# A graph layer on one core: q in two float32r pieces for its spread, x plus beta made in the prologue, and the root from logarithm and exponential

## The chip, the cores and the metric

The kernel runs on one NeuronCore of a Trainium2 chip. The core has a matrix engine (TensorE, "PE", with its weight loads as "PEld"), three other compute engines (VectorE "DVE", ScalarE "ACT", GpSimd "POOL"), a sync engine ("SP") that only issues transfers, and 16 DMA engines. Each engine runs its own instructions in order, and they meet by semaphores. The metric is the device time of one execution in microseconds, as the median of several runs.

## The reference

There are 12500 nodes with 256 features and 200000 edges, sorted by destination. `h` is the normalised and rectified `x`; a layer of attention over the edges, with 8 heads of 32, is made from `h`:

```python
h = jnp.maximum(_layernorm(x, axis=-1), 0.0)
q, k, v = h @ Wq + bq, h @ Wk + bk, h @ Wv + bv      # (n, 8, 32) each
logits = jnp.einsum('ehd,ehd->eh', q[dst], k[src]) / jnp.sqrt(jnp.float32(D))
expv = jnp.exp(logits - jax.ops.segment_max(logits, dst, num_segments=n)[dst])
attn = expv / jax.ops.segment_sum(expv, dst, num_segments=n)[dst]
agg = jax.ops.segment_sum(attn[:, :, None] * v[src], dst, num_segments=n)
y = h + jax.nn.gelu(agg.reshape(n, HID) + (h @ Wskip + bskip), approximate=False)
out = x + (y - mean(y)) / jnp.sqrt(var(y) + 1e-05) * gamma + beta
```

(Two lines are drawn together here; the order of the work is the reference's.)

## The kernel before

**Prologue** (`project`, about the first 200 us). The rows of `x` are loaded in groups of up to four blocks of 128 rows (`load`, L201, five tiles `x_in`, on SP's queue). DVE takes the statistics of each block (L227, L232), ACT their root (L235), DVE its reciprocal and the shift (L239, L240), ACT the normalised rows `h` (L249). After the last block of a group `normalise` stores `h` to `h_tab` (L252) and issues the next load, into the tile that this group leaves. TensorE transposes `h` (L261) and multiplies it with the weights of k and v (L349) into `ps_kv` (four tiles); DVE adds the bias (L357), and a group's rows go to `kv_tab` (L359). Between these, POOL, DVE and ACT work off a plan of the edges (`make_plan`) and smaller tables (`aside`); `pieces` (L126) there splits a bias row into three bf16 rows `b_q3`, `b_s3` and `b_o3`, the last for `beta`.

**Walk** (`walk_streams`). The edges are cut into eight streams, and a step `c` walks three tiles of 128 edges of each. In a step and tile:

- `gather` and `gather_row` (L1504) fetch rows of k and v by 24 indirect DMAs a step, issued by POOL. Each is tied to a place in TensorE's order by `turns`.
- `turn_windows` (L1466, L1470) transposes a window of 64 rows of `h` for each stream; `queries` (L1480 to L1487) makes `q` for it in two parts, in a PSUM tile `ps_hot`, and ACT copies it to `qw`.
- `hot_e` (L1529, L1532) makes a matrix of zeros and ones, `to_e`, from edges to window rows.
- `spread` (L1555) multiplies `to_e` with `qw` in float32, so that each edge has its `q`. Two matmuls of 64 rows each stand side by side in the array. The result, `ps_qe`, has two tiles.
- DVE multiplies `q` with k (`times`, L1566), adds over a head (`total`, L1573), TensorE turns the logits (`turn`, L1592), DVE scans the running maxima (`maxima`, L1604 and L1605), ACT takes the exponential (L1608), TensorE turns back (L1614), DVE weighs v (`weigh`, L1640), and TensorE adds the products of a node (`add_up`, L1663).

The 16 most frequent nodes are done densely (`Dense`, L1820 to L1879) from step 2 to step 50.

**Finishing pairs** (`Pair`). From step 15 on, a step fetches the sums of two blocks of nodes that are done, and the next two steps finish them: division (L1225), the skip product (L1237), the sums added on TensorE (L1242), GELU on ACT (L1246), `h` added and the statistics (L1249 to L1258), the root on ACT (L1262), reciprocal and shift on DVE (L1266, L1267), the normalised rows on ACT (L1272), times gamma (L1306). `shifted` (L1299, L1302) makes `x` plus `beta` in a `ps_hot` tile by a matmul of `b_o3` and two with the identity, and DVE adds it (L1308). The four last pairs (`Half`) are finished after the loop in an order of their own, with `raised` (L1283) in place of `shifted` for some.

**The order** of every engine in the walk is the program's: `keep` chains each instruction behind the one before it on its engine. All PSUM tiles of `turn_windows`, `queries`, `hot_e`, `hot_n`, `shifted`, the dense part and some of `add_up` come from one pool, `ps_hot`, with two tiles. ACT's functions come from tables; `table_of` (L1420) loads one early by an activation on a dummy: GELU, then Sqrt, then Exp for each pair.

## Time and profile before

| | us |
|---|---|
| median of 3 runs | 2697.09 |
| lowest, highest | 2688.44, 2704.12 |
| the profiled execution | 2722.66 |
| its span, first to last instruction | 2721.1 |
| mean granted TensorE clock | 0.833 |
| HBM read, written | 505.52 MB, 81.63 MB |

The profile is of one execution, which took 1% longer than the median of the runs. "Busy" is the time in which an engine works on an instruction; the idle time before an instruction is named with the semaphore event that ended it, and "remote" stands where the profile knows no instruction for that event. The records of matmuls have modelled ends.

### The profile page before, as it was taken

What the parts mean: (1) busy time and instruction counts of PE and PEld (TensorE: products, weight loads), DVE (VectorE), ACT (ScalarE), POOL (GpSimd) and SP (SyncE); (2) the same over time, 40 slices, a digit from 0 to 9 for tenths busy, and PEclk for the clock granted to TensorE, in tenths of its full rate; (3) what the DMA queues carried; (4) which work ended last, traced back from release to release, by engine and by line L of the source; (5) the groups of instructions that cost most, each with busy time, mean ns of one, the idle gap of its engine ahead of it and who ended that gap; (6) DMA issues with size and microseconds to landing.
All of it is one profiled execution on the core that took longest, in us unless ns stands there. A gap on an engine that the chain in (4) does not pass through costs nothing. (4 is left out here: it accounts for less than half of the span.)

```text
span 2721.1 us, 38398 instructions
## 1 busy us (share of the span) xinstructions
PE 2093.9 (77%) x10881; PEld 1272.9 (47%) x10881; DVE 1915.3 (70%) x2373; ACT 1204.8 (44%) x2789; POOL 1591.6 (58%) x1744
## 2 busy tenths in 40 slices
PE   9994667776777778877878877787887777767776
PEld 4443444444444445544544444454554444444444
DVE  8885666666676667767766776666777766777776
ACT  5652233332334445445444544444545444444444
POOL 5457466666666556555555655555555555666664
PEclk9997688888788788878887887878888878887778
DMA  9777566766767677767777777767777776777774
GB/s 351 293 273 220 155 200 207 211 206 207 204 209 214 204 215 224 214 208 232 220 210 206 224 213 208 221 204 207 224 221 212 224 213 203 220 225 222 222 214 113
DMA packets 275205, 589.91 MB, mean 217 GB/s; under 512 B 60643, under 2 KB 133400, under 8 KB 272038
## 3 DMA queue, kind: packets, MB, share of 16 engines
q0 software_dynamic: 125344, 409.89, 51.4%
q1 hardware_dynamic: 148416, 176.36, 20.5%
q8 instruction: 89, 1.46, 0.2%
q10 hardware_dynamic: 1222, 1.11, 0.1%
q14 instruction: 134, 1.10, 0.1%
HBM read 505.52 MB, written 81.63 MB: 216 GB/s over the span
## 5 line engine op out<-in xcount | busy, mean ns | idle before, releaser
L1504 POOL DMA_INDIRECT kv<-kv_tab,idx x1472 | 1401.8, 952 | 981.9 <-issue 335.9
L1555 PE MATMUL ps_qe<-qw,to_e 64*128 64x256 f32 x3040 | 589.3, 501 | 34.1 <-DVE kv L1566 25.4
L1566 DVE TENSOR_TENSOR kv<-ps_qe,kv 128x1024 f32<-128x1024 f32 x380 | 451.5, 1217 | 147.2 <-remote 91.4
L1555 PEld LDWEIGHTS ps_qe<-qw,to_e 64*128 64x128 f32 x3040 | 403.5, 249 | 126.6 <-issue 45.5
L1640 DVE TENSOR_TENSOR vw<-ps_x,kv 128x2048 f32<-128x2048 f32 x188 | 427.0, 2271 | 49.7 <-ACT vw L1629 16.6
L1573 DVE TENSOR_REDUCE L<-kv 128x64 f32<-128x2048 f32 x190 | 433.9, 2283 | 4.8
L1484 PE MATMUL ps_hot<-w_q,hwT 128*128 128x256 f32 x768 | 251.3, 475 | 18.5 <-issue 9.9
L1663 PE MATMUL ps_a<-vw,to_n 128*32 128x264 f32 (+1 forms) x2232 | 228.4, 435 | 44.6 <-issue 25.3
L1532 ACT ACTIVATE to_e<-ps_hot,ones 128x384 f32<-128x384 f32 x256 | 146.9, 581 | 255.1 <-remote 96.9
L1487 ACT COPY qw<-ps_hot 128x256 f32<-128x256 f32 (+1 forms) x128 | 60.6, 474 | 344.0 <-PE ps_hot L1484 113.4
L1484 PEld LDWEIGHTS ps_hot<-w_q,hwT 128*128 128x128 f32 x768 | 165.6, 230 | 86.3 <-ACT hwT L1470 34.0
L1663 PEld LDWEIGHTS ps_a<-vw,to_n 128*32 128x32 f32 (+1 forms) x2232 | 88.7, 125 | 245.9 <-issue 194.3
L349 PE MATMUL ps_kv<-w_kv,hT 128*128 128x512 f32 x392 | 184.3, 593 | 0.7 <-ACT hT L263 0.7
L1420 ACT ACT_TABLE_LOAD x142 | 182.2, 1283 | 2.6
L1529 PE MATMUL ps_hot<-et,near 48*128 48x384 bf16 x256 | 94.1, 368 | 102.1 <-issue 84.8
L1614 PE MATMUL ps_x<-ident,W 64*128 64x64 f32 x189 | 28.9, 270 | 179.4 <-ACT hT L1222 113.9
L1470 ACT COPY hwT<-ps_hot 128x256 f32<-128x256 f32 (+1 forms) x128 | 61.2, 478 | 233.7 <-PE ps_hot L1466 129.5
L1604 DVE TENSOR_TENSOR_SCAN ps_x<-pen,ps_x 64x384 f32<-64x384 bf16 x63 | 60.6, 961 | 147.6 <-PE ps_x L1592 79.2
L1866 DVE TENSOR_TENSOR kv<-ps_hot,kv 128x256 f32<-128x256 f32 x49 | 20.8, 425 | 181.1 <-PE ps_hot L1862 100.3
L1680 ACT COPY kv<-ps_a 1x264 f32<-1x264 f32 x372 | 137.3, 369 | 4.5
L1545 ACT ACTIVATE to_n<-ps_hot,ones 128x384 f32<-128x384 f32 x189 | 108.6, 576 | 62.8 <-PE ps_hot L1542 44.9
L1614 PEld LDWEIGHTS ps_x<-ident,W 64*128 64x128 f32 x189 | 19.2, 161 | 210.6 <-ACT hT L1222 132.0
(437 smaller groups left out, 3029.3 us busy)
## 6 DMA issues: line engine op xcount, KB each, us to landing
kv<-kv_tab,idx POOLq DMA_INDIRECT x1520
kv_tab<-kvo SPq DMA_DIRECT2D x23, 1024.0 KB
hw<-h_tab SPq DMA_DIRECT2D x256, 64.0 KB
table<-sums_w SPq DMA_DIRECT2D x252, 61.9 KB
kv<-h_tab SPq DMA_DIRECT2D x98, 128.0 KB
sums<-table SPq DMA_DIRECT2D x94, 132.0 KB
h<-h_tab SPq DMA_DIRECT2D x94, 128.0 KB
x_f<-in_x_dram SPq DMA_DIRECT2D x94, 128.0 KB
```

The source lines that it names most:

```text
L349: nc.tensor.matmul(ps_kv, hT[:, c, :], w_kv[:, c, :], start=c == 0, stop=c == KC - 1)
L1420: keep(nc.scalar.activation(dummy[:, 1:2], dummy[:, 0:1], function))
L1484: keep(nc.tensor.matmul(ps[:, b, :], g["hwT"][:, b, k, :], w_q[:, k, :], start=False, stop=k == KC - 1, skip_group_check=True))
L1504: ins = nc.gpsimd.indirect_dma_start(out=t[:, s, :], out_offset=None, in_=kv_tab[:, :], in_offset=bass.IndirectOffsetOnAxis(ap=idx[:, s, j ...
L1532: keep(nc.scalar.activation(step[c]["to_e"][:, i, :], ps[:, :CH], AF.Relu, scale=-1.0, bias=ones))
L1545: keep(nc.scalar.activation(step[c]["to_n"][:, j, :], ps, AF.Relu, scale=-1.0, bias=ones))
L1555: keep(nc.tensor.matmul(ps[:, b, a, :], g["to_e"][r, 2 * half + a, j * P:(j + 1) * P], g["qw"][r, (half + a) * half, :], start=True, stop= ...
L1566: keep(nc.vector.tensor_tensor(k, g["qe", half].rearrange("p b a d -> p a b d"), k, op=OP.mult))
L1573: keep(nc.vector.tensor_reduce(g["L"][:, j, :].rearrange("p (s h) -> p s h", s=S), g["kv"][j][:, :, :HID].rearrange("p s (h d) -> p s h d" ...
L1640: keep(engine.tensor_tensor(t[:, :, HEADS:].rearrange("p s (h d) -> p s h d", h=HEADS), wj[:, :, :, None].to_broadcast([P, t.shape[1], HEA ...
L1663: keep(nc.tensor.matmul(ps[at:at + w, :], g["to_n"][:, j, i * P + at:i * P + at + w], g["vw"][j][:, s, :], start=j == 0, stop=j == tiles_o ...
L1680: keep(copy(step[c + 1]["kv"][0][0:1, s, HID - HEADS:], ps[at:at + 1, :]))
```

## The change

Three things are changed.

- **q in two pieces.** `queries` copies `q` to a float32r tile, which keeps fewer bits than float32. A new function, `remainders`, multiplies this piece with minus the identity into the PSUM tile that still holds `q`, so that what the first piece lacks is left, and copies that as a second float32r piece. `to_e` is made in float32r, and `spread` adds up two float32r matmuls in place of each float32 one. `qw` has a tile for each part, with two buffers each. `remainders` stands behind `hot_e(c + 2, 0)` for the first part and behind `hot_e(c + 2, 1)` for the second.
- **x plus beta in the prologue.** Once a group of `x` is normalised, POOL adds `beta` to it in place and stores it to a new table in HBM, `xb_tab`, from its own queue. The walk reads `xb_tab` where it read `x`; `shifted`, `raised`, `b_o3` and the late load of `beta` go.
- **The root.** `root` takes the logarithm and then the exponential of minus half of it, in place of Sqrt and a reciprocal on DVE (`inverse` goes too). Both come from one table, together with the Exp of `maxima`. `table_of` loads a table by its name, without a dummy; a pair has two loads, GELU's and, right behind the GELU, the other.

```diff
@@ normalise
                     nc.sync.dma_start(h_tab[starts[g] * P:(starts[g] + n) * P, :]
                                       .rearrange("(p b) d -> p b d", p=P), h_of[g])
+                    nc.gpsimd.tensor_add(x_in[g], x_in[g],
+                                         beta_all[:, None, :].to_broadcast([P, n, HID]))
+                    nc.gpsimd.dma_start(xb_tab[starts[g] * P:(starts[g] + n) * P, :]
+                                        .rearrange("(p b) d -> p b d", p=P), x_in[g])
                     for _ in range(1 + (g == 1) * (5 - 3)):
                         load()
@@ Pair
         def root(self):
-            self.keep(nc.scalar.activation(self.rstd, self.mv[:, :, 1], AF.Sqrt, bias=eps))
+            self.keep(nc.scalar.activation(self.rstd, self.mv[:, :, 1], AF.Ln, bias=eps))
+            self.keep(nc.scalar.activation(self.rstd, self.rstd, AF.Exp, scale=-0.5))
...
-            self.keep(nc.vector.reciprocal(self.rstd, self.rstd))
...
-        def shifted(self):
-
-            self.xb = hot_ps.tile([P, 2, HID], F32, name="ps_hot")
-            self.keep(nc.tensor.matmul(self.xb, one_row, twice(b_o3), start=True, stop=False,
-                                       skip_group_check=True))
-            for b in range(2):
-                self.keep(nc.tensor.matmul(self.xb[:, b, :], ident, self.x[:, b, :], start=False,
-                                           stop=True, skip_group_check=True))
...
-            self.keep(then.tensor_add(self.y, self.g, self.xb))
+            self.keep(then.tensor_add(self.y, self.g, self.x))
@@ table_of
-            keep(nc.scalar.activation(dummy[:, 1:2], dummy[:, 0:1], function))
+            keep(nc.scalar.preload_act_table_set(name))
+
+        GELU, EXP = "gelu_and_others", "natural_log_exp_and_others"
@@ queries
-                g["qw"] = hold.tile([P, 3, HID], F32, name="qw")
+            g["qw", part] = hold.tile([P, 2, n, HID], F32R, name=f"qw{part}", bufs=QBUFS[part])
...
-            keep(nc.scalar.copy(g["qw"][:, tiles, :], ps))
+            keep(nc.scalar.copy(g["qw", part][:, 0], ps))
+            g["rest"] = ps
+
+        def remainders(c, part):
+
+            g = step[c]
+            ps = g.pop("rest")
+            keep(nc.tensor.matmul(ps, less, g["qw", part][:, 0], start=False, stop=True,
+                                  skip_group_check=True))
+            keep(nc.scalar.copy(g["qw", part][:, 1], ps))
@@ spread
-                for b in range(2):
-                    r = slice(b * WN, (b + 1) * WN)
-                    keep(nc.tensor.matmul(ps[:, b, a, :],
-                                          g["to_e"][r, 2 * half + a, j * P:(j + 1) * P],
-                                          g["qw"][r, (half + a) * half, :], start=True, stop=True))
+                for i in range(2):
+                    for b in range(2):
+                        r = slice(b * WN, (b + 1) * WN)
+                        keep(nc.tensor.matmul(ps[:, b, a, :],
+                                              g["to_e"][r, 2 * half + a, j * P:(j + 1) * P],
+                                              g["qw", half][r, i, a * half, :], start=i == 0,
+                                              stop=i == 1))
@@ the loop of steps
             if before:
                 before.factors()
                 before.normal()
-            if before:
-                before.shifted()
...
             hot_e(c + 2, 0)
+            remainders(c + 2, 0)
...
             if pair:
                 pair.gelu()
+                table_of(EXP)
...
             if pair:
-                table_of(AF.Sqrt)
                 pair.root()
-                table_of(AF.Exp)
             queries(c + 2, 1)
             hot_e(c + 2, 1)
+            remainders(c + 2, 1)
```

The tables, `beta`'s rows and `inverse`/`raised` are changed in the same way behind the loop; a matmul with `less`, minus the identity in float32r, is what `remainders` uses.

More of the change, by code (lines that the diff above doesn't have):

```diff
@@ L30 @@
 F32 = mybir.dt.float32
+F32R = mybir.dt.float32r
 BF16 = mybir.dt.bfloat16
@@ L467, in gnn_kernel @@
         walk_streams(tc, N, HID, NST, KL, many, ident, idx, d0_row, slot_row, near, near_n, e_tab, pen_tab,
[L468 to L469 removed]
+                     h_tab, kv_tab, table, xb_tab, out, w_q, w_s, one_row, b_q3, b_s3,
+                     gam, eps, run_tab, cnt_tab, own, Wk, bk, Wv, bv)
     with branch.Else():
@@ L1113, in walk_streams @@
 def walk_streams(tc, N, HID, NST, KL, many, ident, idx, d0_row, slot_row, near, near_n, e_tab, pen_tab, h_tab,
-                 kv_tab, table, x, out, w_q, w_s, one_row, b_q3, b_s3, b_o3, gam, beta, eps,
+                 kv_tab, table, x, out, w_q, w_s, one_row, b_q3, b_s3, gam, eps,
                  run_tab, cnt_tab, own, Wk, bk, Wv, bv):
@@ L1398, in walk_streams @@
         nc.vector.memset(low0, -BIG)
+        less = one.tile([P, P], F32R, name="less")
+        nc.scalar.activation(less, ident, AF.Copy, scale=-1.0)
         pin = one.tile([P, 2 * P + 2], F32, name="pin")
```

58 lines of the change are left out of this document (19 added, 39 removed).

## The prediction

> **What bounds the kernel now.** I read the page first, its busy shares and its row of granted clock, then the window sums by stage, then VectorE's groups with their waits, and last the timeline of one step.
>
> ```profile
> span 2721.1 us, 38398 instructions
> PE 2093.9 (77%) x10881; PEld 1272.9 (47%) x10881; DVE 1915.3 (70%) x2373; ACT 1204.8 (44%) x2789; POOL 1591.6 (58%) x1744
> 1511.17 0.95 POOL L1504 DMA_INDIRECT kv<-kv_tab,idx  x1 [0.30 <-issue]
> ```
> No engine is full. In the window sums (columns: length, then busy time and count of PE, weight loads, DVE, ACT, POOL, then granted clock, DMA share, GB/s) I take two windows of the prologue, then the steps without a pair of finished blocks, then most of those with one:
>
> ```profile
> 0.00:100.00 100.00, 96.55 (x309) 48.48 (x310) 83.74 (x278) 60.85 (x145) 63.50 (x117) 1.00 0.93 339
> 100.00:200.00 100.00, 100.00 (x330) 48.44 (x328) 84.87 (x267) 61.66 (x144) 44.73 (x68) 1.00 0.77 277
> 347.00:821.00 474.00, 338.98 (x1889) 206.17 (x1881) 315.65 (x248) 159.97 (x416) 295.75 (x313) 0.82 0.70 206
> 821.00:2200.00 1379.00, 1084.34 (x5772) 671.85 (x5772) 978.67 (x1067) 652.25 (x1484) 796.17 (x836) 0.83 0.73 216
> ...
> L1605 DVE TENSOR_TENSOR_SCAN M<-pen,ps_x x14: 954/955/956, 347.3 to 821.0; 64x384 f32<-64x384 bf16 x14
> L1605 DVE TENSOR_TENSOR_SCAN M<-pen,ps_x x36: 954/955/956, 821.0 to 2213.4; 64x384 f32<-64x384 bf16 x36
> ```
> The prologue is TensorE's (96.55 and 100 of 100 us). The scan of L1605 comes once a step, so a step takes 473.7/13 = 36.4 us without a pair and 1392.4/35 = 39.8 us with one. In the last window PE is 79% busy, DVE 71%, and one gather takes 0.95 us of POOL and 0.30 to the next (the timeline's row above: start, length, what, idle before), 24 of them 30 us. So a step is a loop of waits between engines of similar load. DVE has the most work that can't be moved, so I price the change by what it does to DVE's waits. Its groups from 800 to 2400 us (40 steps), busy and mean, then idle time before them:
>
> ```profile
> L1566 DVE TENSOR_TENSOR kv<-ps_qe,kv 128x1024 f32<-128x1024 f32 x244 | 290.0, 1218 | 68.7 <-remote 44.3 <-PE ps_hot L1529 23.4 <-issue 0.9
> L1604 DVE TENSOR_TENSOR_SCAN ps_x<-pen,ps_x 64x384 f32<-64x384 bf16 x40 | 38.5, 961 | 92.0 <-PE ps_x L1592 68.8 <-PE ps_qe L1555 22.2 <-PE ps_hot L1466 0.9
> L1249 DVE TENSOR_TENSOR sums<-sums,h 128x512 f32<-128x512 f32 x39 | 27.0, 693 | 75.9 <-ACT hwT L1470 37.6 <-ACT sums L1246 19.3 <-issue 18.9
> L1306 DVE TENSOR_TENSOR sums<-sums,gam 128x512 f32<-128x512 f32 x38 | 26.3, 692 | 55.0 <-ACT sums L1272 48.8 <-issue 6.2
> L1866 DVE TENSOR_TENSOR kv<-ps_hot,kv 128x256 f32<-128x256 f32 x36 | 15.3, 425 | 124.0 <-PE ps_hot L1862 58.1 <-PE ps_qe L1555 56.5 <-issue 6.2
> ```
> A step waits 1.7 us for gathers and PE (L1566), 2.3 for the scan's transposes (L1604), 1.9 for the GELU's result (L1249), 1.4 for the normalised rows (L1306) and 3.1 for the dense transposes (L1866).
>
> **The change, part by part.** *Beta's matmuls go (L1299, L1302).* One step around the wait for the scan:
>
> ```profile
> 1528.70 0.58 PE L1299 MATMUL ps_hot<-b_o,one_row 3*128 3x512 bf16 x1 [2.36 <-ACT to_e L1532]
> 1529.22 2.07 PE L1302 MATMUL ps_hot<-x_f,ident 128*128 128x256 f32 x4
> 1531.22 3.79 PE L1555 MATMUL ps_qe<-qw,to_e 64*128 64x256 f32 x16
> 1535.28 0.27 PE L1592 MATMUL ps_x<-ident,L 128*64 128x128 f32 x1
> 1535.59 0.96 DVE L1604 TENSOR_TENSOR_SCAN ps_x<-pen,ps_x 64x384 f32<-64x384 bf16 x1 [3.48 <-PE ps_x L1592]
> ...
> L1299 PE MATMUL ps_hot<-b_o,one_row x47: 371/579/604, 893.5 to 2710.8; 3*128 3x512 bf16 x47
> L1302 PE MATMUL ps_hot<-x_f,ident x180: 379/634/796, 893.9 to 2623.6; 128*128 128x256 f32 x180
> ```
> TensorE does beta (0.58 us) and x (2.07), then two spreads (3.79), then the transpose for which the scan has waited 3.48 us. Overlaps taken off, the first two are 2.5 us here; I take 2.2 for the mean step, since the fast form of the records (371 and 379 ns) is also seen. They also hold one of the two ps_hot tiles.
>
> *The spread in float32r (L1555).* What TensorE takes for it:
>
> ```profile
> L1555 PE MATMUL ps_qe<-qw,to_e 64*128 64x256 f32 x3040 | 589.3, 501 | 34.1 <-DVE kv L1566 25.4
> 1511.64 0.73 PEld L1555 LDWEIGHTS ps_qe<-qw,to_e 64*128 64x128 f32 x8 [0.30 <-DVE kv L1566]
> 1511.65 1.13 PE L1555 MATMUL ps_qe<-qw,to_e 64*128 64x256 f32 x8
> ```
> Four calls a spread on 380 spreads make 1520 matmuls, and the trace has 3040: a float32 matmul is two records. A record with 256 float32 columns lasts as long at its shortest as one with 512 bf16 columns (379 and 371 ns), so each record runs at half bf16's pace. No float32r row exists. If a call is one record at bf16's pace, eight calls stand where eight records stood at half the length each: about 0.5 us less of the 1.13 of a spread. If it is one record at the old pace, nothing changes; if it stays two records, a spread costs about 1.0 us more. The weight loads stay eight, 0.73 us, and may then set the pace, so I take 0.3 us a spread, between the first two. Of six spreads in a step, two lie ahead of the scan's transpose and one ahead of L1862. The other three end while DVE does other work and count nothing; if that cover goes, they add 0.9 us to the gain.
>
> *The second piece of q.* Twice a step comes a matmul with minus the identity and a second ACT copy out of the same ps_hot tile.
>
> ```profile
> 1517.47 0.37 ACT L1487 COPY qw<-ps_hot 128x256 f32<-128x256 f32 x1 [5.51 <-remote]
> 1517.74 0.59 ACT L1532 ACTIVATE to_e<-ps_hot,ones 128x384 f32<-128x384 f32 x1
> 1517.90 1.01 PE L1466 MATMUL ps_hot<-ident,hw 128*128 128x128 f32 x4 [2.72 <-ACT qw L1487]
> ...
> 1519.43 0.60 ACT L1246 ACTIVATE sums<-ps_a 128x512 f32<-128x512 f32 x1
> ```
> Now L1466 starts when the first copy is out. Afterwards it also waits for the remainder's matmul, the 0.59 us activation ahead of it on ACT, and a copy like the 0.37 us one: about 0.9 us later. Behind L1466 on TensorE stand the transpose of L1592 and the second half of q; behind its result on ACT stands the GELU (L1246), and DVE's L1249 waits for that, so this 0.9 us is on the path with a pair. The same round trip for the second half stands ahead of the last spread; I put it at nothing with a pair, because qw's copy comes earlier (next part), and at 0.9 if that fails. Bounds for both trips together: nothing, and 3 us (two copies, the matmul near 0.4 us and the handovers, twice).
>
> *The root.* Three table switches a pair become two, and Sqrt with a reciprocal becomes Ln and Exp.
>
> ```profile
> L1420 ACT ACT_TABLE_LOAD x142 | 182.2, 1283 | 2.6
> L1420 ACT ACTIVATE dummy<-dummy 1x1 f32<-1x1 f32 x142 | 28.7, 202 | 1.6
> L1262 ACT ACTIVATE rstd<-mv,eps 128x2 f32<-128x2 f32 x47 | 13.9, 295 | 11.8 <-DVE mv L1258 4.8 <-issue 4.1 <-DVE st L1256 3.0
> L1266 DVE RECIPROCAL rstd<-rstd 128x2 f32<-128x2 f32 x46 | 7.1, 155 | 0.0
> ```
> ACT loses 1.28 us and three dummies of 0.20, and gains one activation near 0.30: 1.6 us less, of which the two new copies (0.37 and 0.59) take back 0.96. The load behind the root is gone, so qw's second copy follows the statistics 1.2 us sooner, and the normalised rows come some 0.3 us earlier for L1306. DVE loses 0.16 us outright. [...]
>
> *The prologue.* All of x gets beta on POOL and is written once more, 12.8 MB, from POOL's queue.
>
> ```profile
> L1283 POOL TENSOR_TENSOR x_f<-x_f,kv x2: 1264/1268/1272, 2661.6 to 2684.4; 128x512 f32<-128x512 f32 x2
> L1362 POOL DMA_DIRECT2D kv<-in_x_dram x16 | 8.5, 553 | 0.3
> L349 PE MATMUL ps_kv<-w_kv,hT 128*128 128x512 f32 x392 | 184.3, 593 | 0.7 <-ACT hT L263 0.7
>   DMA x_in<-in_x_dram: 5.6, 5
> POOL kv L1492 <- PE ps_hot L1529: 16.8, 1, 16.8
> ```
> An addition over 512 columns took 1.27 us, so one over 1024 takes 2.5, and the 25 groups about 62 us, with 25 issues of 0.55 us (14 us). POOL was idle 92 us in the first 200 and waited 16.8 us at the end, so it has room. But a load of x now waits for the addition and the store of the group five before it, 5 us or more behind plan work. The last but one row is from the waits of L227, the statistics: they waited only 5.6 us for such loads, which come just in time; behind a waiting L227 on DVE stand the evictions of L357, and TensorE has four tiles before it stops. Behind the load on SP stand the stores of h and of keys and values. DMA is 0.93 and 0.77 busy. Bounds: nothing, and 12.8 MB at 339 GB/s unhidden, 38 us. I take 12, nearer the free end because four tiles of 1.9 us (184.3 us for 98 blocks) cover one late load.
>
> *The end.* Four additions of 1.27 us on POOL, beta's DMA and the last two pairs' matmuls go: 2 us, between 0 and 8.
>
> **The sum.** With a pair: beta's matmuls 2.2 and two spreads 0.6 make 2.8, but the scan's wait is 2.3, so 2.3; the third spread 0.3, L1306 0.3, the reciprocal 0.16; against them 0.9 at L1249. That is 2.16 off. Gathers are next: their waits (1.1 us of L1566's 1.7) grow as steps shorten, and I give 0.26 back: 1.9. Without a pair: 0.6 + 0.3 off, 0.5 on for round trips without the GELU: 0.4. So 46 x 1.9 = 87, 16 x 0.4 = 6, the end 2, the prologue +12: 83 us less. The profiled execution itself took 2722.7 us (span 2721.1), so 2640 on its scale. The median of the three runs is 2697.09, 26 less; the same 83 us off gives **2614**.
>
> **The rivals.** *TensorE is the real bound* (chance 0.15). For: 79% busy, and only 8.5 us a step left. Then beta's 2.2 and six spreads' 1.8 less two 0.15 us matmuls count in full, 3.7 a pair step and 1.5 otherwise: 46 x 3.7 + 16 x 1.5 = 194, less 12: 2515. Against: the waits of DVE for ACT and gathers do not shrink with it.
>
> *The gathers take it all* (0.12). For: 30 us of POOL and a DMA share of 0.73; 44.3 of L1566's 68.7 us wait is for no engine of the profile. Then steps keep their length and the prologue and the end remain: 2707. Against: steps without a pair run 3.4 us shorter on the same gathers.
>
> *The round trip of q, slower* (0.18). The place is ps_hot with two tiles: TensorE, in order, stands at L1466 and at the last spread while ACT copies, 3 us a step (bound above), and float32r is no faster per record, so the spread gives nothing. Then 62 x 3 = 186 on, against beta's 46 x 2.2 = 101, plus 10 around the loop: 2790. It decides for slower once the trips cost more than about 1.6 us a step (101/62).
>
> *The clock falls* (0.07). With less work TensorE idles more; if its mean fell from 0.83 to 0.77, its 31 us a step would grow by 0.83/0.77 to about 33, and the loop would gain nothing: about 2700. [...] The trace speaks against: 0.82 at 72% busy, 0.83 at 79%.
>
> The change also would not do what it says if a float32r call stays two records; that is the slower rival made worse.
>
> **How the numbers follow.** The forecast has 0.48, alone 2575 to 2655 (1 to 2.7 us a pair step). Faster by over 0.5%, which is about what a measurement of this kernel can tell from no change, gets 0.48 + 0.15 and 0.05 of the gather and clock cases: 0.68. Within 0.5%: 0.12. Slower: 0.20. The range takes in the forecast, the gather and clock cases and most of the TensorE case, 2520 to 2720; the slower rival is left out.
>
> **What would show it.** L1604's wait falls from 2.3 us a step to under 0.5; L1299 and L1302 are gone; the float32r rows number 3040 with half the mean length where eight stand together; L1249 waits longer, near 2.8 us; steps with a pair measure near 38 us, those without 36; the first scan starts some 12 us later. I am wrong if the float32r count is 6080, if L1466 or the last spread waits for ACT over 1.6 us, if L1566's wait for gathers takes the gain, or if the prologue grows by over 38 us.

## The result and the profile after

| | before | after |
|---|---|---|
| median, same chip | 2695.07 (4 runs, 2688.44 to 2704.12) | 2788.68 (4 runs, 2777.92 to 2793.32) |
| the profiled execution's span | 2721.1 | 2791.7 |
| mean granted clock | 0.833 | 0.789 |

The changed kernel is slower: 1.0333 times the time before, 95% interval 1.0298 to 1.0369. The forecast was 2614.

The page after, its header and three of its costliest groups (busy, mean ns of one, then idle time before and what ended it):

```profile
span 2791.7 us, 38306 instructions
PE 2000.6 (72%) x10774; PEld 1211.2 (43%) x10774; DVE 1936.2 (69%) x2321; ACT 1184.3 (42%) x2781; POOL 1654.4 (59%) x1780
L1566 DVE TENSOR_TENSOR kv<-ps_qe,kv 128x1024 f32<-128x1024 f32 x380 | 451.9, 1218 | 237.6 <-PE ps_qe L1554 200.5
L1554 PE MATMUL ps_qe<-qw,to_e 64*128 64x256 f32 x3040 | 387.1, 377 | 45.5 <-issue 19.5
L1483 PE MATMUL ps_hot<-qw,less 128*128 128x256 f32 (+1 forms) x128 | 71.5, 558 | 218.7 <-ACT qw L1476 126.4
```

TensorE works 93 us less and the kernel takes longer. Two rows say when the prologue's matrix work and the first step's scan come, as "first and last start"; first before, then after:

```profile
L349 PE MATMUL ps_kv<-w_kv,hT x392: 592/592/697, 7.2 to 199.5; 128*128 128x512 f32 x196
L1605 DVE TENSOR_TENSOR_SCAN M<-pen,ps_x x63: 954/955/956, 275.5 to 2664.5; 64x384 f32<-64x384 bf16 x63
```

```profile
L356 PE MATMUL ps_kv<-w_kv,hT x392: 592/592/1223, 7.8 to 263.0; 128*128 128x512 f32 x196
L1605 DVE TENSOR_TENSOR_SCAN M<-pen,ps_x x63: 954/955/956, 352.5 to 2737.8; 64x384 f32<-64x384 bf16 x63
```

The last matmul of keys and values comes 63.5 us later, and from it to the first scan it takes 89.5 us in place of 76.0, 13.5 more. From the first to the 63rd scan, 62 steps, it takes 2385.3 in place of 2389.0. But the profiled execution of before lay some 27 us above its median. A better stand-in is the run with the new root alone (e4 below: ratio 0.9994, span 2699.0), whose 62 steps take 2365.4. Against it the walk lost 20 us (18, if each kernel's median is put in place of its profiled execution). From the 63rd scan to the end it takes 53.9 us where it was 56.6, 3 less. So 63.5 + 13.5 + 20 - 3 = 94, against 93.6 between the medians.

**The prologue.** Windows of after (length, then busy time and count of PE, weight loads, DVE, ACT, POOL, then clock, DMA share, GB/s), and below them its waits on SP's queue and DVE (total, times, longest):

```profile
0.00:100.00 100.00, 82.48 (x247) 40.29 (x248) 74.36 (x212) 43.91 (x107) 71.73 (x111) 0.96 0.83 291
100.00:200.00 100.00, 81.97 (x254) 38.68 (x253) 81.88 (x227) 54.30 (x128) 68.80 (x82) 0.94 0.74 275
...
SPq L214 <- DMA xb_tab<-x_in: 160.6, 19, 19.6
DVE st L229 <- DMA x_in<-in_x_dram: 40.9, 12, 10.4
```

TensorE, full before, now idles 18 us in 100. DMA is less busy than before (0.83 and 0.74 against 0.93 and 0.77), so it wasn't bandwidth that ran short. SP's queue stands 160.6 us at loads of `x` that wait for the new stores, and DVE waits 40.9 for those loads, 5.6 before. One group, in the timeline (start, length; the number in brackets is the idle time before):

```profile
119.65 2.34 POOL L256 TENSOR_TENSOR x_in<-x_in,beta_all 128x1024 f32<-128x1024 f32 x1 [0.19 <-ACT h L251]
119.79 2.23 DVE L242 SCALAR_TENSOR_TENSOR nr<-mv,nr 128x4 f32<-128x4 f32 x1
122.28 0.55 POOL L258 DMA_DIRECT2D xb_tab<-x_in  x1 [0.30 <-POOL x_in L256]
126.96 0.33 SPq L214 DMA_DIRECT2D x_in<-in_x_dram  x1
```

The addition takes 2.34 us, the store is issued 0.29 us later, and the load that wants this tile goes out at 126.96, 7.3 us after the addition began. Taken over the 5th to the 20th group, from the starts and ends of L251, L256, L258 and L214: from the end of a group's normalisation 7.2 us until POOL begins to add, 2.35 for the addition, 0.9 until the store has been issued, 4.7 until the next load is issued; 15.2 in all. Before, the load was issued 0.42 us after the normalisation. The statistics began 12.5 us after the issue of their load before, and some 4.1 where the load is what they wait for, so there were 8.4 us to spare; 15.2 is more. Not every load came late: the statistics waited in 12 of the 27 groups.

The second row shows something else: a shift over 128 x 4 elements, 0.2 us before, takes 2.23 and ends 0.03 us after the addition beside it. Its group before and after:

```profile
L240 DVE SCALAR_TENSOR_TENSOR nr<-mv,nr 128x4 f32<-128x4 f32 (+2 forms) x27 | 5.5, 203 | 0.9
```

```profile
L242 DVE SCALAR_TENSOR_TENSOR nr<-mv,nr 128x4 f32<-128x4 f32 (+2 forms) x27 | 20.4, 756 | 0.9
```

Summed over all the lines of DVE that both traces have in equal count up to the first scan, the same instructions take 31 us longer after. DVE was busy 84 of 100 us in the prologue, so this alone is as much as all its idle time in 200 us.

One more wait is in DVE's own order. The last block of `x` has fewer than 128 rows, and DVE sets its tile to zero (L211) as soon as a tile is free. It stood 11.5 us before that one instruction, with the evictions behind it; before, it didn't wait there. So DVE's waits and slower instructions can be added up: 35 us more for loads, 12 for this, 31 for slower instructions, less 11 that it waits less for TensorE (6.5 for 17.8), make 66, for the 63.5 that the prologue lost.

**The walk.** DVE's waits after, 800 to 2400 us (41 steps), against the rows of before in the prediction; and two of TensorE's groups in the same window:

```profile
L1566 DVE TENSOR_TENSOR kv<-ps_qe,kv 128x1024 f32<-128x1024 f32 x246 | 292.6, 1218 | 141.8 <-PE ps_qe L1554 126.8 <-PE ps_hot L1527 8.7 <-issue 3.4
L1604 DVE TENSOR_TENSOR_SCAN ps_x<-pen,ps_x 64x384 f32<-64x384 bf16 x41 | 39.2, 956 | 14.6 <-PE ps_hot L1848 6.1 <-PE ps_hot L1844 3.7 <-PE ps_a L1663 3.6
...
L1554 PE MATMUL ps_qe<-qw,to_e 64*128 64x256 f32 x1970 | 247.6, 372 | 14.9 <-issue 5.8 <-ACT to_e L1530 5.2 <-DVE kv L1566 3.9
L1483 PE MATMUL ps_hot<-qw,less 128*128 128x512 f32 x83 | 45.7, 550 | 165.2 <-ACT qw L1476 105.3 <-issue 56.7 <-ACT rstd L1269 2.0
```

The scan's wait went from 2.3 us a step to 0.4, as forecast. In its place the products of q and k wait 3.5 us a step where it was 1.7, now nearly all for the last spread; ahead of that spread stands the remainder's matmul, for which TensorE sits idle 4.0 us a step. The other waits of the prediction's list hardly move: L1249 1.9 to 2.0, L1306 1.4 to 1.3, L1866 3.1 to 3.5 us a step.

By the scans of M, a step with a pair takes 39.0 us, where before took 39.8 and e4 39.2; a step without one takes 38.0, where both took 36.3 to 36.4. So the walk loses in the steps without a pair. There the clock fell as well; windows before, then after:

```profile
280.00:500.00 220.00, 155.56 (x879) 97.12 (x876) 145.88 (x113) 71.50 (x186) 132.70 (x140) 0.82 0.66 196
500.00:800.00 300.00, 216.52 (x1176) 131.18 (x1176) 197.41 (x157) 101.00 (x263) 186.66 (x198) 0.81 0.69 206
```

```profile
280.00:500.00 220.00, 135.72 (x755) 85.01 (x753) 128.23 (x114) 63.40 (x145) 125.50 (x132) 0.65 0.63 184
500.00:800.00 300.00, 214.90 (x1100) 126.48 (x1100) 187.84 (x146) 101.81 (x262) 175.60 (x186) 0.70 0.67 195
```

### The profile page after: what moved, and what is told of

Same layout as the page of the kernel before. It is cut to its first block, busy times and chain, and to the rows that moved or that the text cites. A ratio compares the mean times of both kernels' runs of the same rounds, so it can differ in the third digit from the quotient of the medians.

```text
span 2791.7 us, 38306 instructions
## 1 busy us (share of the span) xinstructions
PE 2000.6 (72%) x10774; PEld 1211.2 (43%) x10774; DVE 1936.2 (69%) x2321; ACT 1184.3 (42%) x2781; POOL 1654.4 (59%) x1780
## 5 line engine op out<-in xcount | busy, mean ns | idle before, releaser
L1554 PE MATMUL ps_qe<-qw,to_e 64*128 64x256 f32 x3040 | 387.1, 377 | 45.5 <-issue 19.5
L1554 PEld LDWEIGHTS ps_qe<-qw,to_e 64*128 64x128 f32 x3040 | 307.6, 250 | 120.3 <-issue 66.0
L1663 PE MATMUL ps_a<-vw,to_n 128*32 128x264 f32 (+1 forms) x2232 | 268.4, 504 | 121.7 <-issue 78.3
L1530 ACT ACTIVATE to_e<-ps_hot,ones 128x384 fp32r<-128x384 f32 x256 | 148.3, 582 | 222.1 <-PE ps_hot L1527 157.7
L1476 ACT CAST qw<-ps_hot 128x256 fp32r<-128x256 f32 (+1 forms) x128 | 61.1, 478 | 405.7 <-remote 220.0
L1483 PE MATMUL ps_hot<-qw,less 128*128 128x256 f32 (+1 forms) x128 | 71.5, 558 | 218.7 <-ACT qw L1476 126.4
L356 PE MATMUL ps_kv<-w_kv,hT 128*128 128x512 f32 x392 | 198.5, 632 | 38.0 <-DVE kvo L364 31.6
L1866 DVE TENSOR_TENSOR kv<-ps_hot,kv 128x256 f32<-128x256 f32 x49 | 20.8, 425 | 198.6 <-PE ps_hot L1862 183.4
L1244 PE MATMUL ps_a<-w_s,hT 128*128 128x256 f32 x368 | 143.7, 558 | 0.0
L1483 PEld LDWEIGHTS ps_hot<-qw,less 128*128 128x128 f32 x128 | 29.6, 232 | 252.7 <-ACT qw L1476 138.1
L1244 PEld LDWEIGHTS ps_a<-w_s,hT 128*128 128x128 f32 x368 | 99.9, 286 | 38.1 <-issue 19.1
```

Of the source, the lines that this page charges most:

```text
L356: nc.tensor.matmul(ps_kv, hT[:, c, :], w_kv[:, c, :], start=c == 0, stop=c == KC - 1)
L1244: self.keep(nc.tensor.matmul(self.ps[:, b, :], self.hT[:, b, c, :], w_s[:, c, :], start=False, stop=False, skip_group_check=True))
L1530: keep(nc.scalar.activation(step[c]["to_e"][:, i, :], ps[:, :CH], AF.Relu, scale=-1.0, bias=ones))
L1554: keep(nc.tensor.matmul(ps[:, b, a, :], g["to_e"][r, 2 * half + a, j * P:(j + 1) * P], g["qw", half][r, i, a * half, :], start=i == 0, sto ...
L1663: keep(nc.tensor.matmul(ps[at:at + w, :], g["to_n"][:, j, i * P + at:i * P + at + w], g["vw"][j][:, s, :], start=j == 0, stop=j == tiles_o ...
```

## The experiments

Each ratio is to the kernel before on the same chip, with its 95% interval. The chips are A (e1 to e4, before 2696 us), B (e5, e6, e8, e9; 2720), C (e7, e10 to e12; 2718) and D (e13 to e18; 2187 to 2189, more on it below). "kv" is the last matmul of keys and values, "scan" the first scan of M, "walk" the 62 steps from it, all in us from profiled executions; these lie up to 1% off their medians (e5 23 us, e1 14 and e6 13 below, e13 12 and e7 9 above), and B and C run 22 to 24 us slower than A, so a difference of 20 us between two walks says little, and less between two chips.

| | kernel | ratio | kv | scan | walk | clock |
|---|---|---|---|---|---|---|
| e1 | the change without x plus beta | 1.0137 (1.0083 to 1.0191) | 201.4 | 291.1 | 2365.5 | 0.801 |
| e2 | x plus beta alone | 1.0037 (1.0010 to 1.0064) | 263.0 | 344.1 | 2306.6 | 0.836 |
| e3 | two pieces of q alone | 1.0195 (1.0143 to 1.0247) | 199.6 | 289.5 | 2395.8 | 0.785 |
| e4 | the root alone | 0.9994 (0.9965 to 1.0022) | 200.0 | 276.3 | 2365.4 | 0.826 |
| e5 | e3, no remainders | 0.9902 (0.9868 to 0.9937) | 200.3 | 269.0 | 2343.5 | 0.782 |
| e6 | e3, TensorE filled | 1.0258 (1.0208 to 1.0309) | 200.9 | 288.8 | 2429.6 | 0.797 |
| e7 | e3, second remainder later | 1.0160 (1.0097 to 1.0223) | 200.0 | 291.4 | 2424.5 | 0.781 |
| e8 | e2, six tiles `x_in` | 1.0016 (0.9990 to 1.0041) | 254.3 | 335.1 | 2325.1 | 0.833 |
| e9 | e2, a tile for the sum | 1.0193 (1.0143 to 1.0243) | 301.1 | 388.0 | 2334.0 | 0.819 |
| e10 | beta added in the walk | 1.0051 (1.0020 to 1.0083) | 203.5 | 288.8 | 2382.6 | 0.824 |
| e11 | e2, stores only | one run, 2704.65 | 241.3 | 320.6 | 2326.9 | 0.831 |
| e12 | e2, additions only | one run, 2715.79 | 240.9 | 320.8 | 2336.6 | 0.829 |
| e13 | e3, remainders' copies only | 1.0068 (1.0045 to 1.0091) | 204.2 | 260.3 | 1900.3 | 0.863 |
| e14 | e3, remainders' matmuls only | 1.0158 (1.0129 to 1.0188) | 200.3 | 263.8 | 1889.0 | 0.886 |
| e15 | one piece of q | 1.0273 (1.0242 to 1.0305) | 200.4 | 257.1 | 1927.1 | 0.811 |
| e16 | e8, additions cut in four | 1.0292 (1.0271 to 1.0313) | 250.5 | 305.2 | 1892.2 | 0.910 |
| e17 | e3 again | 1.0153 (1.0091 to 1.0215) | 200.3 | 265.7 | 1888.2 | 0.898 |
| e18 | e15 again | 1.0269 (1.0230 to 1.0308) | 200.0 | 257.1 | 1931.1 | 0.807 |

### The parts by themselves (e1 to e4)

The edits are those of the diff above, in whole parts: e1 leaves out "x plus beta in the prologue", and e2, e3 and e4 make one part each on the kernel before.

> The changed kernel with x plus beta put back where it was (shifted, raised, b_o3, the late load of beta); q in two pieces and the new root stay. Theory A (the whole loss is the prologue: x_in is held until POOL's addition and the store are done; the walk as a whole loses nothing): the first scan comes at about 276 us as before, not 352, and the steps without a pair return to about 36.4 us, because the clock of 0.70 to 0.77 after the stalled prologue is what made them 38.9; the time is near 2700 (2680 to 2720). Rival B (the two pieces of q cost 2.5 us a step by their round trip through ACT, whatever the clock, and beta's matmuls gone had paid for it): first scan at 276, steps without a pair stay near 38.9, steps with one come to about 42; the time is near 2830.

> The kernel before with x plus beta in the prologue alone. Theory A: the first scan is 70 to 80 us late (346 to 356 us), the steps with a pair gain up to 2 us once the clock is back, the time is 2700 to 2770. Rival B: first scan equally late, but steps with a pair gain 3 us, 138 in all, so 2630. Rival D (the late prologue came from the three changes together, not from x plus beta): first scan at 276 to 290, time 2600 to 2660.

> The kernel before with q in two float32r pieces alone. Theory A: first scan at about 276; steps without a pair 36 to 36.5 us at a clock of 0.82, steps with one 39 to 40; the time is within 20 us of 2695. Rival B (round trip): steps without a pair 38.9, those with one 42; time near 2850. The forecast's own figure for this part (0.6 to 0.9 off, 0.9 on a step) gives no change within 20 us.

> The kernel before with the new root and the two table loads a pair alone. The forecast's figure is 0.3 us (L1306) and 0.16 us (the reciprocal) a step with a pair, 21 us in all: near 2674. Rival: ACT has the time anyway, and the time stays within 10 us of 2695. The prologue and the steps without a pair do not change under either.

**The prologue's loss is x plus beta alone**: kv is at 263.0 in e2 as in after, and at 200 to 201 in the other three. The 13.5 us between kv and the first scan belong to the two pieces: 89.9 and 89.7 us in e3 and e1, 76.3 in e4.

**x plus beta does gain in the walk.** e2's walk is 59 us shorter than e4's, 1.25 us for each of 47 steps with a pair, within theory A's 2 and far from rival B's 3. DVE's waits in e2, 800 to 2400 us (42.5 steps):

```profile
L1557 DVE TENSOR_TENSOR kv<-ps_qe,kv 128x1024 f32<-128x1024 f32 x255 | 303.2, 1218 | 96.9 <-remote 64.4 <-PE ps_hot L1520 24.8 <-PE ps_qe L1546 7.7
L1595 DVE TENSOR_TENSOR_SCAN ps_x<-pen,ps_x 64x384 f32<-64x384 bf16 x43 | 41.2, 958 | 15.9 <-PE ps_qe L1546 3.9 <-PE ps_hot L1457 3.9 <-PE ps_x L1583 2.4
```

The scan's wait is gone (0.4 us a step), and the products' wait grew from 1.7 to 2.3. The steps without a pair, where no beta is added, take 36.3 us in e2 and in e4; those with one 37.7 and 39.2. The gain just doesn't pay for the prologue.

**The two pieces lose** 2%, less than rival B's 2850 and more than theory A's 20 us: 13.5 us at the start and 30 in the walk. Nearly all of the 30 lies in the steps without a pair, 38.0 us each for e4's 36.3; with one they take 39.5 for 39.2. **The root** by itself changes nothing: the 0.46 us a step that I had for it aren't there. On top of the two pieces it may be worth something, since e1 lies 0.6% below e3, but their intervals overlap. And the parts don't add up: x plus beta costs 0.4% alone and 1.9% on top of the others (1.0333 over 1.0137). e1's waits, 800 to 2400 us, point to the reason:

```profile
L1575 DVE TENSOR_TENSOR kv<-ps_qe,kv 128x1024 f32<-128x1024 f32 x249 | 296.4, 1218 | 115.8 <-PE ps_qe L1563 71.5 <-PE ps_hot L1536 28.8 <-remote 9.6
L1613 DVE TENSOR_TENSOR_SCAN ps_x<-pen,ps_x 64x384 f32<-64x384 bf16 x42 | 40.2, 958 | 25.3 <-PE ps_x L1601 16.5 <-PE ps_hot L1853 4.4 <-PE ps_hot L1901 2.6
```

With the faster spreads the scan waits only 0.6 us a step. Taking beta's matmuls away there wins little more of that wait, and the products' wait grows by 0.7 us a step (115.8 over 41.5 steps to 141.8 over 41). Theory A fell in its second half: the walk isn't neutral in each part, but has a gain of 59 us and a loss of 30 that together lose 20.

### The second piece (e5, e6, e7)

e5 leaves `remainders` out; the spreads issue as many matmuls, with the first piece twice, so the second is left out. e6 and e7 keep the result.

```diff
 e5
-            remainders(c + 2, 0)
...
-            remainders(c + 2, 1)
...
-                                              g["qw", half][r, i, a * half, :], start=i == 0,
+                                              g["qw", half][r, 0, a * half, :], start=i == 0,
 e6, in hot_e
+            for _ in range((3, 7, 1, 1)[i] if c > 1 else 1):
                 keep(nc.tensor.matmul(ps[:, :CH], near[:, i * P:(i + 1) * P], step[c]["et"],
 e7
-            remainders(c + 2, 1)
             next(making, None)
             spread(c + 1, K - 1, 1)
-            hot_e(c + 2, 2)
             add_up(c, 0, range(K - 1))
+            remainders(c + 2, 1)
+            hot_e(c + 2, 2)
```

> The kernel before with q in float32r, but the second piece left out: no remainders, and each spread uses the first piece twice, so that it issues as many matmuls as with two pieces (q is then rounded to one piece). It stands against the run with two pieces and nothing else changed (2748 us, steps without a pair 38.0 us at a mean clock of 0.72). Theory R (the round trip through ACT is the cost: TensorE waits at the remainder, and what stands behind it comes late): steps without a pair back to 36.5 or less, time 2680 to 2700. Theory C (TensorE's clock is the cost: the shorter spreads leave it idle stretches, and the clock stays low): the remainder's matmuls gone make it idle even more, so the clock stays at 0.78 or less and the time within 20 us of 2748.

> The kernel before with q in two float32r pieces, and idle TensorE filled: the matmul of hot_e for part 0 is issued 3 times and that for part 1 7 times into the same tile, ahead of the two remainders, where TensorE waits for ACT's copy of q (3.3 us ahead of the second in the step shown by the trace). The result is the same. That is 8 matmuls of 0.33 to 0.50 us, some 3 us more of TensorE a step. Theory C: fewer stretches at clock 0.5, mean clock 0.82 or more, steps without a pair about 37, time 2700 to 2725. Theory R: the wait for ACT is filled, nothing else changes, 2748 within 10 us; if the wait is not really idle (the ends of matmuls are modelled), up to 3 us a step more, 2750 to 2900.

> The kernel before with q in two float32r pieces, and the second remainder moved behind the last spread and behind add_up of the first two tiles (it belongs to the next step's q, which nothing needs so soon); TensorE has that work to do while ACT copies the first piece. It stands against a ratio of 1.0195 with the remainder ahead of them, and 0.990 with no remainders. Theory R (what costs is that the last spread and add_up stand behind the wait for ACT): ratio 1.000 to 1.008, the wait of the last spread's DVE product falls. Rival H (two more copies and matmuls in one of the two ps_hot tiles cost wherever they stand, because the tile is held longer): 1.015 to 1.025.

e5 is 3% below e3, each against the kernel before on its own chip: 20.5 us earlier at the first scan and 52 us less in the walk, 0.84 a step. That is theory R (steps without a pair take 36.7 us, where it had 36.5 or less). So on these chips the remainders are the loss, and without them the faster spreads are worth 1%, 27 us, of which 7 lie at the start. The clock doesn't explain it here: e5's, 0.770 to 0.786 over its executions, is no higher than e3's (0.781 to 0.785), and e5 is the fastest. Windows of the steps without a pair, e3 and then e5:

```profile
347.00:821.00 474.00, 344.81 (x1849) 202.60 (x1849) 303.13 (x239) 166.05 (x423) 285.36 (x301) 0.73 0.68 197
```

```profile
347.00:821.00 474.00, 337.29 (x1873) 206.61 (x1873) 312.70 (x247) 160.59 (x416) 292.43 (x310) 0.72 0.69 204
```

At the same clock DVE gets 3% more done in e5. e6 fills TensorE's wait and doesn't raise the clock where it was low (0.72 from 347 to 821 us); over the whole run the clock is 0.797 for 0.785, under theory C's 0.82, and the time is not the 2700 to 2725 of that theory. Its walk is 34 us longer, but on a chip that is 24 slower; by the ratios it loses 0.6% to e3, with intervals that overlap. In e7 the last spread no longer stands behind the second remainder, and yet the ratio stays within e3's interval: rival H by its number. The products' wait does fall, to 1.3 us a step where e3 has 3.1, but the scan's wait is back at 2.0 where e3 has 0.9. That this place in the order was the cost is refuted: the wait only moved. What in the remainder it is, e13 and e14 ask.

### The prologue taken apart (e8, e9, e11, e12, e16)

```diff
 e8
-                xt = pool.tile([P, 4, HID], F32, name="x_in", bufs=5)[:, :n, :]
+                xt = pool.tile([P, 4, HID], F32, name="x_in", bufs=6)[:, :n, :]
...
-                    for _ in range(1 + (g == 1) * (5 - 3)):
+                    for _ in range(1 + (g == 1) * (6 - 3)):
 e9
+                    xb = pool.tile([P, 4, HID], F32, name="xb", bufs=1)[:, :n, :]
-                    nc.gpsimd.tensor_add(x_in[g], x_in[g],
+                    nc.gpsimd.tensor_add(xb, x_in[g],
 e11 (x itself is stored; the result lacks beta)
-                    nc.gpsimd.tensor_add(x_in[g], x_in[g],
-                                         beta_all[:, None, :].to_broadcast([P, n, HID]))
 e12 (the walk reads x; the result lacks beta)
-                    nc.gpsimd.dma_start(xb_tab[starts[g] * P:(starts[g] + n) * P, :]
-                                        .rearrange("(p b) d -> p b d", p=P), x_in[g])
 e16, on e8, for each block in place of each group
+                nc.gpsimd.tensor_add(x_in[g][:, b, :], x_in[g][:, b, :], beta_all)
```

> The kernel before with x plus beta in the prologue alone, and six tiles x_in in place of five. In the trace a group's next load is issued 15.2 us after the group is normalised (7.2 until POOL begins to add, 2.35 the addition, 0.9 until the store is issued, 4.7 until it has landed), against 0.4 us before, and the load had 8.4 us to spare; a sixth tile gives one group's time more, 7.8 us. Theory A (the tile is held too long): the last matmul of keys and values starts at 200 to 215 us, not 263, the first scan at 280 to 295, and the walk keeps its gain; time 2630 to 2655. Rival D (the 12.8 MB of stores take the DMA's time, whatever the number of tiles): the last such matmul stays at 235 us or later, time 2680 or more.

> The kernel before with x plus beta in the prologue alone, but POOL writes the sum into a tile of its own (one buffer) and stores from there, so that x_in is free at the end of the addition and not at the landing of the store: 9.5 us after the group is normalised in place of 15.2, against 8.4 to spare. Theory A: the last matmul of keys and values at 205 to 225 us, time 2635 to 2665. Rival D (DMA): as with six tiles, 235 us or later, time 2680 or more. Rival P (POOL's own queue: the addition comes late behind the plan's work, 7.2 us in the mean and 20 at the worst, so the store hardly matters): 230 to 250 us, time 2665 to 2690.

> The kernel before with the new table written in the prologue, but without POOL's additions: x itself is stored and read back, so the result lacks beta. Theory N (the additions are the cost: while POOL adds, DVE's short instructions take longer, 23 to 31 us on the same instructions in the runs with additions, and POOL's own order makes the release of x_in late): the last matmul of keys and values at 200 to 215 us, the first scan at 275 to 295. Rival D (the 12.8 MB of stores and their wait): 235 us or later.

> The kernel before with POOL's additions in the prologue, but without the stores: the walk reads x, and the result lacks beta. Theory N: the last matmul of keys and values at 235 us or later, DVE's same instructions 20 us or more longer. Rival D: 200 to 215 us.

> The kernel before with x plus beta in the prologue alone, six tiles x_in, and POOL's addition cut into one per block of 128 rows (128 x 256, 0.73 us in the trace in place of 2.35), each behind its own normalised block. Theory L (a DVE instruction that meets an addition waits for its end): the same DVE instructions take less than 12 us longer in place of 23, the last matmul of keys and values comes at 215 to 235 us in place of 254, ratio 0.985 to 0.995 in place of 1.0016. Rival (POOL's total of work and its order are what counts; 98 additions are 71 us where 27 are 58): 250 us or later, 1.00 or more.

**Both halves cost the same.** Stores alone put kv at 241.3, additions alone at 240.9, both together at 263.0: 41 us each and 63 together, so theory N and rival D were each half wrong. Both hold the tile of `x`: SP's queue stands at the loads for the stores in e11, and for the additions in e12.

```profile
SPq L212 <- DMA xb_tab<-x_in: 119.3, 18, 15.3
```

```profile
SPq L211 <- POOL x_in L253: 107.2, 19, 16.5
```

Only the additions slow DVE's instructions, as its shift shows, e11 and then e12:

```profile
L240 DVE SCALAR_TENSOR_TENSOR nr<-mv,nr 128x4 f32<-128x4 f32 (+2 forms) x27 | 5.9, 218 | 0.9
```

```profile
L239 DVE SCALAR_TENSOR_TENSOR nr<-mv,nr 128x4 f32<-128x4 f32 (+2 forms) x27 | 21.9, 810 | 0.9
```

DVE's same instructions take 32 us longer in e12, 1 in e11. DVE's rows add up here too. In e11, 40 more for loads, 11 before the zeroing, 1 for slower instructions and 8 less for TensorE make 44. In e12, 20 for loads, 5 for the zeroing, 32 for slower instructions, 1 for a tile and 14 less for TensorE make 44. Each lost some 41. So the additions act by both ways, and the stores by the held tile alone.

**A longer buffer doesn't mend it.** e8 wins 9 us of 63, where theory A had 48 or more. The loads are early again there (12.7 us from issue to statistics, as before), but DVE's waits moved to the next queue; e8, up to 270 us, on SP's queue and on DVE:

```profile
SPq L212 <- DMA xb_tab<-x_in: 145.4, 19, 19.7
...
DVE kvo L362 <- DMA kv_tab<-kvo: 22.1, 4, 6.9
DVE x_in L209 <- DMA xb_tab<-x_in: 18.6, 1, 18.6
```

SP still stands 145 us at the loads, the stores of keys and values stand behind them, and so the evictions of DVE wait for their tile. The last row is the one instruction that sets the last tile to zero: DVE stood 18.6 us before it, for the store that still held the tile, and everything behind it on DVE stood too. With 23 us of slower instructions, and 9 that it waits less for TensorE, DVE's rows make 55, and e8 is 55 behind at kv. e9 came out on the wrong side, 38 us worse than e2. Its tile for the sum has one buffer, and now POOL itself, with the plan behind it, waits:

```profile
POOL xb L255 <- DMA xb_tab<-xb: 90.2, 17, 8.2
```

My figure of 9.5 us of hold had left that wait out. e16 eases the slow instructions (DVE's same instructions 14 us longer in place of 23, where theory L had under 12; the shift's mean 393 ns) and kv comes at 250.5, 4 us earlier than e8: theory L is nearly right about the instructions, the rival about the time. Of the 50 us that are left, DVE's rows show 16 for the tile of keys and values, 19 before the zeroing, 14 for slower instructions and 3 for loads, less 4. No run moved the zeroing or the loads out of the way, so what each would win is open. e16's ratio was measured on chip D and isn't to be set beside e8's: it lost 64 us there, more than the 50 of the prologue, so the gain of x plus beta in the walk that e2 showed on chip A isn't seen on D.

### Beta in the walk (e10)

```diff
-                before.shifted()
+                before.raised(beta_all)
```

> The kernel before, with beta added to x by POOL in the walk, once per finished pair (128 x 512, 1.27 us), in place of the three matmuls of shifted; no second table, the prologue as before. Theory W (the walk's gain of the change comes from TensorE's beta matmuls going, 1.3 to 1.8 us a step with a pair in the run with x plus beta alone): the first scan at about 275 us, steps with a pair 1 to 1.7 us shorter, ratio 0.972 to 0.985. Rival: POOL's addition makes the gathers late and DVE's short instructions long, as the additions did in the prologue (a 0.2 us instruction took up to 2.9): ratio 0.99 to 1.00.

No gain, as the rival had it; the ratio lies just above its range. The scan's wait falls as in e2, but the normalised rows are late now; its groups, 800 to 2400 us:

```profile
L1596 DVE TENSOR_TENSOR_SCAN ps_x<-pen,ps_x 64x384 f32<-64x384 bf16 x42 | 40.1, 956 | 14.8 <-PE ps_hot L1458 6.0 <-remote 5.6 <-PE ps_qe L1547 1.7
L1298 DVE TENSOR_TENSOR sums<-sums,gam 128x512 f32<-128x512 f32 x39 | 27.0, 691 | 136.1 <-ACT sums L1273 133.1 <-issue 3.0
```

1.4 us became 3.5 there, and the products' wait fell to 0.6 us a step. The rival's reasons don't show: the wait for gathers fell as well, and the two short instructions of DVE that make the factors for the normalisation take 154 and 166 ns, 155 and 178 before. Only the addition of `h` (L1250) takes longer, 812 ns for 693, which is 0.12 us a step. So the wait has moved from the scan and the products to the normalised rows; what makes these late wasn't taken apart. The start is late too, the first scan by 13 us against e4, which is not explained.

### Which half of the remainder, and one piece (e13, e14, e15, e17, e18)

```diff
 e13: remainders without (the second piece is q again)
-            keep(nc.tensor.matmul(ps, less, g["qw", part][:, 0], start=False, stop=True,
-                                  skip_group_check=True))
 e14: remainders without (the spreads use the first piece twice)
-            keep(nc.scalar.copy(g["qw", part][:, 1], ps))
 e15, e18: no remainders, one matmul in spread (the second piece is left out)
-                for i in range(2):
...
+                                          g["qw", half][r, 0, a * half, :], start=True, stop=True))
```

> The kernel before with q in two float32r pieces, but remainders without its matmul: ACT copies the same q twice, at the same two places, and TensorE does not wait for the first copy (the second piece is then q again, not what the first lacks). It stands between a ratio of 1.0195 with remainders and 0.990 without. Theory M (TensorE's wait for ACT and the matmul are the cost): 0.990 to 1.000. Rival H (ACT's second copy, and the ps_hot tile held until it is done, are the cost): 1.010 to 1.020.

> The kernel before with q in two float32r pieces, but remainders without its copy: TensorE still waits for the first copy and multiplies, and the spreads use the first piece twice. Theory M: 1.010 to 1.020. Rival H: 0.990 to 1.000.

> The kernel before with q in one float32r piece: no remainders, and one float32r matmul where float32 has one, so half the matmuls of the spread (q keeps fewer bits). It stands against 0.990 with the same matmul issued twice. If the spread's length still sets the steps, 3 of 6 spreads at 0.3 to 0.5 us make some 60 to 90 us: 0.96 to 0.97; if the spread is hidden by now, 0.985 to 0.990.

> The kernel before with q in two float32r pieces alone, once more, beside e18_one on one chip. The chips differ: the kernel before took 2696 to 2720 us on three of them and 2189 on a fourth, where the clock is 0.93 in place of 0.82 and where copies alone gave 1.007, the matmul alone 1.016. On a chip like the three: 1.015 to 1.025, clock 0.78. On one like the fourth, Theory M (the matmul and TensorE's wait) gives 1.015 to 1.030; if the copy's cost and the matmul's add up, 1.02 to 1.03.

> The kernel before with q in one float32r piece and half the matmuls, once more: 1.027 at a clock of 0.81 on the fourth chip. On a chip like the three, where the same matmuls issued twice gave 0.990 at a clock of 0.775: Theory C (less work for TensorE lowers its clock, and the rest of its work pays) gives 0.995 to 1.03 at a clock under 0.76; Theory S (the spread's length is on the path) 0.96 to 0.985. On one like the fourth, 1.027 again.

All five ran on chip D. There the matmul with its wait gives 1.0158 and the whole remainder 1.0153, as **theory M** has it; the copies alone give 1.0068, above its range of 0.990 to 1.000 and under rival H's, and add nothing to the matmul. What the remainder costs on D isn't measured, since e5 did not run there. And e15 and e18, with no remainders and half the matmuls, are the slowest of the five, 1.027 twice, which neither case of e15 had foreseen. Windows and two groups of e17 (two pieces), then of e18 (one), 800 to 2100 us:

```profile
800.00:2100.00 1300.00, 1094.66 (x7071) 681.75 (x7070) 1177.94 (x1285) 820.32 (x1862) 980.95 (x1019) 0.92 0.93 277
...
L1567 PE MATMUL ps_qe<-qw,to_e 64*128 64x256 f32 x2026 | 198.8, 312 | 21.1 <-DVE kv L1579 21.1
L1239 PE MATMUL ps_a<-w_s,hT 128*128 128x256 f32 x336 | 95.6, 433 | 0.0
```

```profile
800.00:2100.00 1300.00, 1095.02 (x5799) 659.08 (x5800) 1142.59 (x1247) 760.52 (x1728) 940.49 (x984) 0.81 0.90 268
...
L1555 PE MATMUL ps_qe<-qw,to_e 64*128 64x256 f32 x988 | 144.9, 364 | 10.9 <-DVE kv L1566 10.9
L1239 PE MATMUL ps_a<-w_s,hT 128*128 128x256 f32 x329 | 137.3, 589 | 0.0
```

TensorE is busy 1095 us in both. With 1272 fewer records of matmuls the clock fell from 0.92 to 0.81, and an untouched matmul, the skip product, went from 433 to 589 ns. What the spread saved, the rest of TensorE's work took. On chip D this fits theory C, but no run there raised the clock by itself, and what sets the clock isn't shown; DVE's longer waits in e18, against e17, are for the scan's transposes (31 us for 4), the dense transposes (32 for 15), the GELU's result (50 for 27) and gathers (10 for 1), and its shorter ones for the last spread (3 for 27) and the normalised rows (1 for 23). On A to C e5 spoke against the theory. Why e5's low clock did no harm there stays open, since one piece and no remainders were not run on the same chip as e5.

No version here beats the kernel before and still computes all of q: e5 leaves out the second piece.

## Why the prediction was wrong, step by step

- **What bounds the kernel** (a loop of waits): right, and it is why the gains didn't add.
- **Beta's matmuls, 2.2 us:** the mechanism was right. L1604's wait fell under 0.5, and x plus beta alone won 1.25 us a step on chip A, where 2.2 less 0.26 for the gathers was forecast; the products' wait took 0.6.
- **float32r:** one record a call, 3040 of them, as forecast; 377 ns where it was 501. TensorE spends 3.2 us a step less on it (377 to 248 us of busy time in 40 steps). Worth in time: 20 of e5's 27 us lie in the walk, 0.3 a step, where 0.6 to 0.9 was forecast.
- **The round trip, 0.9 us:** in the walk it is 0.84 (e3 against e5), so its size came out, but by luck, since the place was wrong. I had it behind L1466 and on L1249 with a pair, and the second trip at nothing there. L1249's wait stayed at 2.0 us a step in place of 2.8; TensorE's idle time is at the remainder's matmul, 4.0 us a step, and DVE's wait at the last spread behind it. And the steps without a pair, where I had 0.4 us off, took 1.7 more than e4's. I had not counted the start either, 20.5 us, where four remainders stand with little to cover them.
- **The root, 0.46 us:** 0.9994 by itself, no gain.
- **The prologue, 12 us, bounds 0 to 38: this step failed most.** It took 63.5. I bounded it by bandwidth, and DMA was not short. "Four tiles of 1.9 us cover one late load" was the wrong question: the tile came free 15.2 us after the normalisation against 8.4 to spare, group after group, and the statistics waited 12 times. I gave POOL's additions no price on DVE, where they cost 31 us, and overlooked that DVE itself waits for a free tile to set it to zero, 12 us. (There are 27 groups, not 25, which changes little.)
- **The sum: this step failed as well.** I took 2.3 (the cap of the scan's wait) and then let the gathers have 0.26. The wait that took its place was the last spread, 1.8 us a step more. The rival "the gathers take it all" gave the right size for the walk (no gain) from the wrong wait. Its 2707 with the prologue and start as measured, 63.5 + 13.5 for 12, would be 2772.
- **The slower rival's 2790** lies within 2 us of the measured median, by luck. It had the walk 85 us longer and the prologue and the loop's ends 10, with float32r no faster; the walk lost 20, the prologue and the start 77, and float32r was faster.
- **The clock rival** had 0.07. The clock did fall, to 0.789, most in the steps without a pair; on chip D it fell to 0.81 beside a saving that brought nothing (e18).

I named the sign that came true, "if the prologue grows by over 38 us", but gave it no share of the range. The sign of the round trip, "if L1466 or the last spread waits for ACT over 1.6 us", pointed beside the place: neither does (L1466's matmul waits 0.5 us a step, the spreads 0.4), but the remainder's matmul waits for ACT 2.6 us a step.

## What to carry to other kernels

Before moving work into a stage that is full, follow the buffer it holds: the time from its last old use to its release, against the time the next load has to spare. See which other instructions wait for that buffer, and what stands behind them on their engine. Count what an addition on POOL does to DVE beside it (31 us here), not only POOL's free time. And where two changes shorten the same wait, price the second after the first, by the wait that will then be longest.

## What the runs showed of the hardware

**Beside POOL's addition, DVE's shift lasts until the addition ends.** It took 164 ns at the median before. In after, 9 of its 27 instructions ran beside an addition and ended 0.01 to 0.04 us after it, so they took 0.26 to 3.16 us; the other 18 took 0.16 to 0.17, but for one of 0.46. Not every short instruction is slowed: the reciprocal ahead of the shift took 0.15 to 0.18 us, beside an addition or not. Over the prologue DVE's same instructions take 31 us longer, and e12 against e11, 32 to 1, puts it on the additions. Why the shift waits isn't shown.

**Chips differ by a fifth.** The kernel before takes 2696, 2720 and 2718 us on A, B and C, and 2188 on D, at a clock of 0.93 in place of 0.82 to 0.83. The prologue is the same (kv at 200 us in e4 on A and e18 on D), but the two pieces' walk is 1888 us in e17 and 2396 in e3, 30.5 us a step and 38.6. In the trace of before TensorE sits idle in the walk for no releaser that the trace knows; from 821 to 1800 us such waits are 94 us in 71 places, the first line here the largest:

```profile
PE ps_hot L1529 <- issue: 38.5, 15, 4.7
PE ps_x L1592 <- issue: 11.9, 13, 2.1
```

In e3, on A, they are 72 us in 81 places. In e17, the same kernel on D, the same window has none. They are only a part of the 8 us a step between the two, and what stops TensorE there is open.
